# Late mix, joint biases, and weights placed behind the gathers in a four-stage float32 megakernel

## The chip, the cores and the metric

The kernel runs on one core of one Trainium2 chip, as one launch. The time is the device time in microseconds (us) of that core. In the text TensorE is the matrix engine (PE in the profile, PEld its weight loads), VectorE is DVE, ScalarE is ACT, GpSimd is POOL and SyncE is SP, which issues most transfers.

## The reference

Two layers, each a condition network and a feed-forward network with a residual. There are 32 sequences of 128 tokens of width 512, that is 4096 rows. In short:

```python
# L0_cond: two shared matrices and a routed mixture, 8 experts, two per token
shared = (silu(x @ sw1.T) * (x @ sw3.T)) @ sw2.T
hid = (shared + sum over the two chosen e of gate_e * gelu(x @ rw1[e].T) @ rw2[e].T) / 3
# L0_ffn: one expert of 8 for each SEQUENCE, chosen from its last row
sel = argmax(softmax(gelu(hid[:, -1] @ Wp1 + bp1) @ Wp2 + bp2))
r = gelu(hid @ W1[sel] + b1[sel]) @ W2[sel] + b2[sel]
x = x + hid + 0.3 * (r @ Wo + bo)
# L1_cond: mix with the row before, 16 experts by a hash of the token, at most 256 rows each
xprev = rows of x moved down by one, the condition row first
xk = x + (xprev - x) * time_maa_k
xr = x + (xprev - x) * time_maa_r
y = rows of (relu(xk[expert's rows] @ w_key[e]) ** 2) @ w_value[e], put back by token
z = sigmoid(xr @ w_recept.T) * y
# L1_ffn: a recurrence over the 32 sequences (128 tokens side by side)
for t in range(32):
    f, i = sigmoid(z[t] @ wf.T + c @ uf.T + bf), sigmoid(z[t] @ wi.T + c @ ui.T + bi)
    g = tanh(z[t] @ wc.T + c @ uc.T + bc)
    c = f * c + i * g
out = x + tanh(z @ wo.T + c @ uo.T + bo)
```

All is float32. Each matrix product is made of three products of a high and a low part (high by high, high by low, low by high). So every operand is first split: ScalarE casts to the high part (line 63) and VectorE subtracts it to get the low part (line 64).

## The kernel before

**Order.** The program is written as tiles and instructions. A planner fixes each engine's order ahead of the run, from the order in which the program is written and its own estimate of durations; what is written first comes first where both are ready by that estimate. On the chip each engine then takes its instructions in that fixed order. `with tc.issue_after(i)` keeps the instructions written inside it that run on i's engine behind i; it says nothing of other engines. `behind(both)` does so for a pair, one of ScalarE and one of VectorE. `last_split` is the pair of the latest split. A tile pool with `bufs=n` gives n places to tiles of one tag; a tile waits until the place's last user is done, and pools opened later reuse the memory of closed ones.

**Stages.** Up to 300 us: the shared network of the first half of the groups, and the router. Then the routed experts by row blocks, to 560. Then the shared network of the second half (`shared`, L215), in which `combine` (L747) puts the parts together and stores hid. In its last group, after chunk 0, `policy` (L770) chooses the expert of each of the first 24 sequences and sorts them by expert. The first three weights of the next stage are fetched then (`fetch_w`, L859, an indirect gather on POOL), and split in the last three chunks by `hook2` (L939 to 948). Each split is followed by the fetch of the weight three places on, which needs the place of the split one.

**The sequence feed-forward loop** (L1178 to 1237) runs over b from -1 to 32, a sequence b per iteration, with up one block ahead and the rest behind. In iteration b TensorE makes `up(b+1, "a")` (pu), `turn_r(b-1)` (pr: transposes of the finished block), `down(b, "a")` (po), `bend(b+1, "a")` (pt: transposes, then gelu with bias into hf, split into hb), `up(b+1, "b")`, `down(b, "b")`, `bend(b+1, "b")`. `used()` after each product runs `split_w`, inside a condition that is false where the expert stays the same, and fetches the next. `turn_r` adds the bias b2 to pr in PSUM, four 128-column pieces, each once on ScalarE (L1079) and once on VectorE (L1080). In odd iterations `send_k` transposes xk (ptB) and stores its rows; after `down(b, "b")` and after `bend(b+1, "b")` come two `send_v` (pv: xr by w_recept, then the rows are stored to v_d). In even iterations `close` (L1086) multiplies by Wo (pb), adds the residual, makes x1, dx and xk for two sequences, and `mix_r` (L1134) makes xr from dx directly after. Transposes pt, pr, ptB and pth share two PSUM banks (`ps_t`, L976); pb and pv share three. Four late `combine` (pth) and a second `policy` for the last 8 sequences run between iterations 3 and 17. Stores to xk_d and v_d have row addresses that are known only in the run, so each waits for the landing of the one before to the same array.

After the loop come the last `send_k` and `send_v`, with all stores on SyncE.

**The hashed experts** (L1245 to 1387): 16 experts of 8 weight pieces. `fetch_rows` gathers each expert's rows of xk from memory (rowsD), once all xk are stored; `turn_rows` transposes (ptD) and splits them. phD and poD are the two products. The results go to res_d.

**The recurrence** (from L1390): `get_y` gathers y by token from res_d on POOL and loads the gate product r from v_d; `gate_y` multiplies, transposes (ptF) and splits to z; `from_c` and `from_x` make the three gates' products. Its weights come through `weight` (L1373): two halves loaded into staging tiles, then split. uf is loaded on SyncE, wc, wi and wf on ScalarE's queue, into a staging pool of four 4 KB tiles that lies behind the recurrence weights. Eight result tiles (zok) are kept in a pool of their own.

Of the kernel before, what the change touches and what calls it, by code (L numbers as in the profile page):

```python
# [48 lines left out]
def tile_kernel(ctx: ExitStack, tc: tile.TileContext, a: dict, out: bass.AP):  # L49
# [106 lines left out]
    with ExitStack() as sa:  # L156
# [718 lines left out]
        def bias_of(kind, b, o):  # L875
            return bcol[b][:, BIAS[kind] * KD + o : BIAS[kind] * KD + o + 1]
# [21 lines left out]
        with ExitStack() as s2:  # L898
# [65 lines left out]
    with ExitStack() as sb:  # L964
# [37 lines left out]
        def seq(p):  # L1002

            if p not in seqs:
                seqs[p] = nc.sync.value_load(seq_i[0:1, p : p + 1], min_val=0, max_val=PARTS[where(p)[0]] - 1)
            return seqs[p]

        def rows_of(t, p):

            return t[bass.ds((seq(p) + where(p)[0] * PARTS[0]) * P, P), :]  # L1010
# [58 lines left out]
        def turn_r(b):  # L1069
# [7 lines left out]
            for o in range(KD):  # L1077
                hi = rTs[c][:, 0, o, bass.ts(j, P)]
                done_a = nc.scalar.activation(hi, pt[:, o, :], AF.Identity, bias=bias_of("W2a", b, o))  # L1079
                done_v = nc.vector.scalar_tensor_tensor(  # L1080
                    rTs[c][:, 1, o, bass.ts(j, P)], pt[:, o, :], bias_of("W2a", b, o),
                    hi.bitcast(F32), ALU.add, ALU.subtract,
                )
            return done_a.ins, done_v.ins
# [63 lines left out]
        def send_k(b):  # L1148
# [5 lines left out]
            done = nc.scalar.copy(rows, pt.rearrange("p k q -> p (k q)"))  # L1154
            nc.sync.dma_start(out=rows_of(xk_d, b), in_=rows)
            return done.ins
# [21 lines left out]
        for b in range(-1, NB + 1):  # L1178
            c, j = divmod(b - 1, PB)
            if b + 1 < NB:  # L1180
# [28 lines left out]

            pair = b - 3 if b % 2 and 0 <= b - 3 < NB - 2 else None  # L1210
# [15 lines left out]
            if pair is not None and pair < NB - 6:  # L1226
                send_v(pair)
            if b + 1 < NB:
                bend(b + 1, "b")
            if pair is not None and pair < NB - 6:  # L1230
                send_v(pair + 1)
            if j == PB - 1 and 0 <= c < NB // PB:
                wo_done, k_done = close(c, b == NB)
                fetch_xh(c + 1)
                if c < NB // PB - 2:
                    mix_r(c, bp, "xr")
                elif c == NB // PB - 2:
                    mix_r(c, end_p, "xr")
# [3 lines left out]
        for b in range(NB - 2, NB):  # L1242
            rows_done = send_k(b)
# [11 lines left out]
    with ExitStack() as sd:  # L1255
# [97 lines left out]
        for p in range(NPC):  # L1353
# [14 lines left out]
            if p == NPC - 9:  # L1368
# [4 lines left out]
                def weight(name, pool, stage, bufs, tag="raw", parts=2, queue=nc.sync):  # L1373

                    pair = pool.tile([P, 2, KD * D], FR, tag=name, name=f"{name}_hl")
# [14 lines left out]
    with sf:  # L1390
        kw = dict(reuse_waits="tile")
        ZS = 2
        uf_p = sf.enter_context(tc.tile_pool(name="uf_p", bufs=1, side="right", **kw))
# [12 lines left out]
        def get_y(b):  # L1406

            y = yp.tile([P, D], F32, tag="y", name=f"y_{b}")
            nc.gpsimd.indirect_dma_start(  # L1409
# [5 lines left out]
            ys[b] = (y, r)  # L1415

        LEAD = 2
        for b in range(LEAD):
            get_y(b)
# [3 lines left out]
        def gate_y(b):  # L1423
# [11 lines left out]
            split(zs[g][:, 0, :, s], zs[g][:, 1, :, s], pt)  # L1435
# [9 lines left out]
        def from_x(t, ps, which, start, stop):  # L1445
            g, j = divmod(t, GB)
            for n in which:
                if start:
                    ps[n] = ps_g.tile([P, D], F32, tag="g", name=f"ps_{n}_{t}")
                mm3(ps[n], lambda h, k: zs[g][:, h, k, bass.ts(j, P)], lambda h, k: wx[n][:, h, k, :], KD, start, stop)  # L1450

        def from_c(t, n, ps, cT, start, stop):
            if start:
                ps[n] = ps_g.tile([P, D], F32, tag="g", name=f"ps_{n}_{t}")
            mm3(ps[n], lambda h, k: cT[:, h, k, :], lambda h, k: uc[n][:, h, k, :], KD, start, stop)
# [16 lines left out]
        def unit(n, k0=0, k1=KD):  # L1472
# [15 lines left out]
            elif g >= NG - 1 - ZS:  # L1488
                zos[g, o] = zop.tile([P, GT], F32, name=f"zok_{g}_{o}")
# [37 lines left out]
        with tc.tile_pool(name="stage", bufs=4, side="right", **kw) as stage:  # L1527
            uc["f"] = weight("uf", uf_p, stage, 4)
# [198 lines left out]
```

## Time and profile before

| what | value |
|---|---|
| median of 3 runs | 2526.67 us (2520.85 to 2529.47) |
| the profiled execution | 2522.89 us, span 2521.2 us |
| TensorE busy | 2455.6 us (97%) |
| VectorE, ScalarE busy | 1331.5 us (53%), 1064.6 us (42%) |
| mean granted clock of TensorE | 0.989 |
| transfers | 351.11 MB, mean 139 GB/s |

The page lists busy time and instructions of each engine. A wait is listed as who waited, for whom, the total, how often and the longest. In a listing by time, a row has the start, the length from the first to the last instruction merged in it, the engine, line, operation, output and inputs, sizes and count; idle time of the engine before it and what ended it stand in brackets. A stage row has the window, its length, and for each engine the busy time and instructions, then the granted clock, the share of the transfer engines and GB/s.

### The profile page before, as it was taken

Reading aid. Unit: us, or ns where it says so; the run is one execution under the profiler, and the core shown is the slowest. Engines: PE = TensorE matmul, PEld = TensorE weight load, DVE = VectorE, ACT = ScalarE, POOL = GpSimd, SP = SyncE. Lnnn points to the kernel's source line nnn. Section 1 sums busy time; section 2 is a strip of 40 time slices with the busy share of each in tenths; the row PEclk is TensorE's granted clock in tenths of the full one; section 3 lists DMA queues with packets and bytes.
Section 4 is the critical chain, followed back from the end, with each engine's and each line's share of the span. In section 5 each row is a group of like instructions: output and inputs, shape, how many; then the busy total and the mean of one; then the engine's idle time right before and its main releaser. Section 6 shows DMA issues by size and latency. Waiting matters only on the chain. (4 is left out here: it accounts for less than half of the span.)

```text
span 2521.2 us, 37055 instructions
## 1 busy us (share of the span) xinstructions
PE 2455.6 (97%) x13044; PEld 2074.9 (82%) x13044; DVE 1331.5 (53%) x2341; ACT 1064.6 (42%) x1935; POOL 429.6 (17%) x460
## 2 busy tenths in 40 slices
PE   8999999999999899999999999999999999999996
PEld 5688899987888788888887889999978888888885
DVE  7797644556567444444454477667643323333336
ACT  4444533343223555455455466666532212222224
POOL 1000022222233333323223010000010000000003
PEclk9999999999999999999999999999999999999998
DMA  5545544457565333342342387776441111111027
GB/s 180 165 125 168 180 151 154 156 184 249 176 217 168 113 107 127 116 134 70 104 146 96 123 295 226 231 234 224 139 160 42 38 38 38 43 42 42 25 80 267
DMA packets 193117, 351.11 MB, mean 139 GB/s; under 512 B 37473, under 2 KB 72337, under 8 KB 189857
## 3 DMA queue, kind: packets, MB, share of 16 engines
q1 hardware_dynamic: 141504, 244.42, 29.6%
q0 software_dynamic: 36160, 74.90, 10.3%
q10 hardware_dynamic: 15264, 29.37, 3.2%
q8 instruction: 108, 1.77, 0.3%
q14 instruction: 81, 0.66, 0.1%
HBM read 373.94 MB, written 88.13 MB: 183 GB/s over the span
## 5 line engine op out<-in xcount | busy, mean ns | idle before, releaser
L64 DVE TENSOR_TENSOR wD<-rawD,wD 128x1024 fp32r<-128x1024 f32 x128 | 156.4, 1229 | 77.4 <-ACT wD L63 77.2
L81 PE MATMUL p<-xhl,swu 128*128 128x512 f32 x768 | 188.0, 396 | 5.5 <-ACT xhl L63 5.5
L81 PEld LDWEIGHTS phD<-xe,wD 128*128 128x128 f32 x1536 | 184.6, 189 | 1.2
L81 PE MATMUL phD<-xe,wD 128*128 128x256 f32 x1536 | 185.3, 281 | 0.0
L81 PE MATMUL p<-xhl,kept_u 128*128 128x512 f32 x768 | 184.3, 394 | 0.7 <-DVE kept_u L64 0.7
L81 PE MATMUL poD<-wD,hD 128*128 128x512 f32 x768 | 181.3, 392 | 0.0
L81 PEld LDWEIGHTS p<-xhl,swu 128*128 128x128 f32 x768 | 143.8, 189 | 36.0 <-ACT xhl L63 5.8
L81 PEld LDWEIGHTS p<-xhl,kept_u 128*128 128x128 f32 x768 | 141.8, 188 | 30.1 <-DVE kept_u L64 1.1
L81 PEld LDWEIGHTS poD<-wD,hD 128*128 128x128 f32 x768 | 142.0, 188 | 28.4
L63 ACT CAST wD<-rawD 128x1024 fp32r<-128x1024 f32 x128 | 133.1, 1046 | 53.4 <-PE poD L81 48.7
L278 POOL DMA_INDIRECT xg<-in_x_rows_dram,blk_t x71 | 67.6, 952 | 463.4 <-PE ptx L288 257.8
L1409 POOL DMA_INDIRECT y<-res_d,gat_i x32 | 33.3, 1040 | 573.9 <-DVE r L1428 495.2
L81 PE MATMUL pur<-r,xb 128*128 x852 | 118.2, 288 | 0.7 <-DVE xb L64 0.4
L81 PE MATMUL por<-r,hbr 128*128 x426 | 116.3, 407 | 1.4 <-ACT hbr L63 1.3
L64 DVE TENSOR_TENSOR xb<-ptx,xb 128x512 fp32r<-128x512 f32 x71 | 49.1, 692 | 115.3 <-ACT xb L63 115.3
L81 PEld LDWEIGHTS pur<-r,xb 128*128 128x128 f32 x852 | 105.2, 189 | 1.7 <-ACT xb L63 0.7
L81 PE MATMUL ps_f<-wf_hl,z 128*128 128x512 f32 x384 | 96.5, 399 | 0.0
L81 PE MATMUL poF<-z,wo_hl 128*128 128x512 f32 x384 | 96.4, 399 | 0.0
L81 PE MATMUL acc<-swd,as 128*128 128x512 f32 x384 | 96.0, 395 | 0.0
L81 PE MATMUL ps_c<-wc_hl,z 128*128 128x512 f32 x384 | 95.1, 395 | 0.7 <-ACT z L63 0.7
L81 PE MATMUL pb<-rT,Wo_hl 128*128 128x256 f32 x768 | 94.6, 281 | 0.0
L81 PE MATMUL pv<-w_recept_hl,xr 128*128 128x512 f32 x384 | 94.3, 395 | 0.0
(1014 smaller groups left out, 5038.3 us busy)
## 6 DMA issues: line engine op xcount, KB each, us to landing
rawD<-in_w_key_dram SPq DMA_DIRECT2D x64, 512.0 KB, 4.1
rawD<-in_w_value_dram SPq DMA_DIRECT2D x64, 512.0 KB, 3.8
swr<-in_sw_dram SPq DMA_DIRECT2D x120, 256.0 KB, 3.7
o_d<-obr SPq DMA_DIRECT2D x71, 256.0 KB, 2.4
xraw<-in_x_dram SPq DMA_DIRECT2D x32, 256.0 KB, 3.8
rraw<-in_rw_dram SPq DMA_DIRECT2D x32, 256.0 KB, 3.4
xc<-in_x_dram SPq DMA_DIRECT2D x32, 256.0 KB, 3.5
hid_d<-o ACTq DMA_DIRECT2D x32, 256.0 KB, 2.2
```

What stands on the lines that cost most here:

```text
L63: first = nc.scalar.copy(hi, src).ins
L64: done = nc.vector.tensor_tensor(lo, src, hi.bitcast(F32), ALU.subtract).ins
L81: done = nc.tensor.matmul(ps, lhsT=left(hl, k), rhs=right(hr, k), start=start and k + n == 0, stop=stop and 3 * k + n == last,)
L278: nc.gpsimd.indirect_dma_start(out=xg[i], out_offset=None, in_=a["x_rows"], in_offset=bass.IndirectOffsetOnAxis(ap=blk_t[:, i : i + 1], ax ...
L1409: nc.gpsimd.indirect_dma_start(out=y, out_offset=None, in_=res_d, in_offset=bass.IndirectOffsetOnAxis(ap=gat_i[:, b : b + 1], axis=0),)
```

## The change

1. `hook2`: the first three weight splits run in chunks 4, 5 and 6 of the last group, before in 5, 6 and 7.
2. `turn_r`: one VectorE add of all four bias columns into the tile `ps`, then a normal split of the whole block.
3. `mix_r(c)` moves from after `close(c)` to the next odd iteration, behind the split of hb.
4. The two `send_v` of a pair move from the odd iteration to the next even one, around `turn_r` and `down(b, "a")`.
5. `send_k` of the last two sequences issues its stores on ScalarE; later ScalarE work of the tail waits behind that issue, before behind the copy of the rows. The row address is loaded into a register of the issuing engine.
6. Recurrence: a pool of four 4 KB tiles (`zop`) is opened first and serves as staging and later for pairs of zok. The tiles of wi, wf, wc are placed in the order i, f, c. Load order is wc, uf, wi on SyncE, before uf on SyncE and wc, wi, wf on ScalarE. wf is loaded on POOL behind the second gather of y. `gate_y` is no longer held behind wc's first part. The f product of t=0 stays behind c and i, and wo's splits behind z.
7. Two late `load_part` (three transfers) stand inside `issue_after(late)`.

```diff
-                    if c >= KF - AHEAD:
+                    if 4 <= c < 4 + AHEAD:
                         with behind(act_split):
-                            split_w(c - KF + AHEAD)
+                            split_w(c - 4)
...
-            for o in range(KD):
-                hi = rTs[c][:, 0, o, bass.ts(j, P)]
-                done_a = nc.scalar.activation(hi, pt[:, o, :], AF.Identity, bias=bias_of("W2a", b, o))
-                done_v = nc.vector.scalar_tensor_tensor(
-                    rTs[c][:, 1, o, bass.ts(j, P)], pt[:, o, :], bias_of("W2a", b, o),
-                    hi.bitcast(F32), ALU.add, ALU.subtract,
-                )
-            return done_a.ins, done_v.ins
+            rT = ps.rearrange("p (k q) -> p k q", k=KD)
+            bias = bias_of("W2a", b, 0, KD).unsqueeze(2).to_broadcast([P, KD, P])
+            nc.vector.tensor_tensor(rT, pt, bias, ALU.add)
+            s = bass.ts(j, P)
+            split(rTs[c][:, 0, :, s], rTs[c][:, 1, :, s], rT)
+            return tuple(last_split)
...
-            done = nc.scalar.copy(rows, pt.rearrange("p k q -> p (k q)"))
-            nc.sync.dma_start(out=rows_of(xk_d, b), in_=rows)
-            return done.ins
+            nc.scalar.copy(rows, pt.rearrange("p k q -> p (k q)"))
+            return queue.dma_start(out=rows_of(xk_d, b, queue), in_=rows).ins
...
+            gated = b - 4 if b % 2 == 0 and 0 <= b - 4 < NB - 6 else None
+            if gated is not None:
+                send_v(gated)
             if 0 <= b - 1 < NB:
                 r_done = turn_r(b - 1)
             if 0 <= b < NB:
                 down(b, "a")
                 used()
+            if gated is not None:
+                send_v(gated + 1)
...
+            if j == 0 and 0 < c < NB // PB:
+                with behind(last_split) if b + 1 < NB else nullcontext():
+                    mix_r(c - 1, end_p if c == NB // PB - 1 else bp, "xr")
...
-            if pair is not None and pair < NB - 6:
-                send_v(pair)
             if b + 1 < NB:
                 bend(b + 1, "b")
-            if pair is not None and pair < NB - 6:
-                send_v(pair + 1)
             if j == PB - 1 and 0 <= c < NB // PB:
                 wo_done, k_done = close(c, b == NB)
                 fetch_xh(c + 1)
-                if c < NB // PB - 2:
-                    mix_r(c, bp, "xr")
-                elif c == NB // PB - 2:
-                    mix_r(c, end_p, "xr")
...
-            rows_done = send_k(b)
+            rows_done = send_k(b, nc.scalar)
...
+        zop = sf.enter_context(tc.tile_pool(name="zop", bufs=4, side="right", **kw))
         uf_p = sf.enter_context(tc.tile_pool(name="uf_p", bufs=1, side="right", **kw))
...
-        with tc.tile_pool(name="stage", bufs=4, side="right", **kw) as stage:
-            uc["f"] = weight("uf", uf_p, stage, 4)
-            for b in range(LEAD):
-                nc.scalar.activation(ys[b][1], ys[b][1], AF.Sigmoid)
-            for n in "cif":
-                from_c(0, n, ps, cT, True, False)
-            wx["c"] = weight("wc", wx_p, stage, 4, queue=nc.scalar)
-            with tc.issue_after(first_part["wc"]):
-                gate_y(0)
-                gate_y(1)
-            for b in range(LEAD):
-                get_y(b + LEAD)
-            for n in "if":
-                wx[n] = weight("w" + n, wx_p, stage, 4, queue=nc.scalar)
-        zop = sf.enter_context(tc.tile_pool(name="zop", bufs=1, **kw))
+        wx_hl = {n: wx_p.tile([P, 2, KD * D], FR, tag="w" + n, name=f"w{n}_hl") for n in "ifc"}
+        wx["c"] = weight("wc", wx_p, zop, 4, pair=wx_hl["c"])
+        uc["f"] = weight("uf", uf_p, zop, 4)
+        wx["i"] = weight("wi", wx_p, zop, 4, pair=wx_hl["i"])
+        for b in range(LEAD):
+            nc.scalar.activation(ys[b][1], ys[b][1], AF.Sigmoid)
+        for n in "cif":
+            from_c(0, n, ps, cT, True, False)
+        gate_y(0)
+        z_done = gate_y(1)
+        with tc.issue_after(first_got):
+            wx["f"] = weight("wf", wx_p, zop, 4, pair=wx_hl["f"], queue=nc.gpsimd)
+        for b in range(LEAD):
+            get_y(b + LEAD)
...
-                from_x(0, ps, "cif", False, True)
-                wo1 = weight("wo", keep_p, yp, 2, "zo", KD)
+                done = from_x(0, ps, "ci", False, True)
+                with tc.issue_after(done):
+                    from_x(0, ps, "f", False, True)
+                with tc.issue_after(z_done):
+                    wo1 = weight("wo", keep_p, yp, 2, "zo", KD)
...
-                load_part(first_p, "c0", "x", 3, 0)
-                load_part(first_p, "cT0", "x", 3, 1, 2)
+                with tc.issue_after(late):
+                    load_part(first_p, "c0", "x", 3, 0)
+                    load_part(first_p, "cT0", "x", 3, 1, 2)
```

More of the change, by code (lines that the diff above doesn't have):

```diff
@@ L873, in fetch_w, with bias_of @@
                     )
-        def bias_of(kind, b, o):
-            return bcol[b][:, BIAS[kind] * KD + o : BIAS[kind] * KD + o + 1]
+        def bias_of(kind, b, o, n=1):
+            return bcol[b][:, BIAS[kind] * KD + o : BIAS[kind] * KD + o + n]
         def split_w(i):
@@ L1000, in tile_kernel, with seq, rows_of @@
         seqs, end_p = {}, None
[L1002 to L1010, printed above, removed]
+        def seq(p, queue=nc.sync):
+            if (p, queue) not in seqs:
+                seqs[p, queue] = queue.value_load(
+                    seq_i[0:1, p : p + 1], min_val=0, max_val=PARTS[where(p)[0]] - 1
+                )
+            return seqs[p, queue]
+        def rows_of(t, p, queue=nc.sync):
+            return t[bass.ds((seq(p, queue) + where(p)[0] * PARTS[0]) * P, P), :]
         xs = {}
@@ L1146, in mix_r, with send_k @@
             split(xrs[c][:, 0], xrs[c][:, 1], dx)
-        def send_k(b):
+        def send_k(b, queue=nc.sync):
             c, j = divmod(b, PB)
@@ L1371, in tile_kernel, with weight @@
                 uc, first_part = {}, {}
-                def weight(name, pool, stage, bufs, tag="raw", parts=2, queue=nc.sync):
-                    pair = pool.tile([P, 2, KD * D], FR, tag=name, name=f"{name}_hl")
+                def weight(name, pool, stage, bufs, tag="raw", parts=2, queue=nc.sync, pair=None):
+                    if pair is None:
+                        pair = pool.tile([P, 2, KD * D], FR, tag=name, name=f"{name}_hl")
                     flat = a[name].rearrange("p k n -> p (k n)")
@@ L1408, in get_y @@
             y = yp.tile([P, D], F32, tag="y", name=f"y_{b}")
-            nc.gpsimd.indirect_dma_start(
+            got = nc.gpsimd.indirect_dma_start(
                 out=y, out_offset=None, in_=res_d,
@@ L1415, in get_y @@
             ys[b] = (y, r)
+            return got.ins
         LEAD = 2
         for b in range(LEAD):
-            get_y(b)
+            first_got = get_y(b)
         zp = sf.enter_context(tc.tile_pool(name="zp", bufs=2, **kw))
@@ L1434, in gate_y @@
             s = bass.ts(j, P)
-            split(zs[g][:, 0, :, s], zs[g][:, 1, :, s], pt)
+            return split(zs[g][:, 0, :, s], zs[g][:, 1, :, s], pt)
         def turn(c, t):
@@ L1449, in from_x @@
                     ps[n] = ps_g.tile([P, D], F32, tag="g", name=f"ps_{n}_{t}")
-                mm3(ps[n], lambda h, k: zs[g][:, h, k, bass.ts(j, P)], lambda h, k: wx[n][:, h, k, :], KD, start, stop)
+                done = mm3(ps[n], lambda h, k: zs[g][:, h, k, bass.ts(j, P)], lambda h, k: wx[n][:, h, k, :], KD, start, stop)
+            return done
         def from_c(t, n, ps, cT, start, stop):
@@ L1454, in from_c @@
                 ps[n] = ps_g.tile([P, D], F32, tag="g", name=f"ps_{n}_{t}")
-            mm3(ps[n], lambda h, k: cT[:, h, k, :], lambda h, k: uc[n][:, h, k, :], KD, start, stop)
+            return mm3(ps[n], lambda h, k: cT[:, h, k, :], lambda h, k: uc[n][:, h, k, :], KD, start, stop)
         def gate(t, n, ps, v, bias):
@@ L1488, in unit @@
             elif g >= NG - 1 - ZS:
-                zos[g, o] = zop.tile([P, GT], F32, name=f"zok_{g}_{o}")
+                if o % 2 == 0:
+                    zok = zop.tile([P, 2, GT], F32, tag="raw", name=f"zok_{g}_{o}")
+                    zos[g, o], zos[g, o + 1] = zok[:, 0, :], zok[:, 1, :]
                 nc.scalar.copy(zos[g, o], po)
@@ L1554, in tile_kernel @@
                 for n in "cif":
-                    from_c(t, n, ps, cT, False, True)
+                    late = from_c(t, n, ps, cT, False, True)
                     gate(t, n, ps, v, bias)
```

## The prediction

> **What bounds the kernel now.** I read the page, then TensorE's own waits, then the busy time by stage, then the order of time on each engine around every wait. The page first:
>
> ```profile
> span 2521.2 us, 37055 instructions
> PE 2455.6 (97%) x13044; PEld 2074.9 (82%) x13044; DVE 1331.5 (53%) x2341; ACT 1064.6 (42%) x1935; POOL 429.6 (17%) x460
> ```
>
> TensorE is busy in all but 2521.2 - 2455.6 = 65.6 us. Its last matmul ends 21.6 us before the span does, so 44 us are gaps inside. Nothing in the change takes away a matmul, so the gain is in gaps. TensorE's waits, who waited for whom (total, times, longest):
>
> ```profile
> PE pt_0a L1050 <- ACT ue_0a L1043: 7.0, 1, 7.0
> ...
> PE ptD L1304 <- DMA rowsD<-xk_d,slot_t: 3.9, 3, 1.7
> ...
> PE ptF L1433 <- DVE z L64: 2.9, 1, 2.9
> PE pt_6a L1050 <- ACT o L756: 2.6, 1, 2.6
> PE ptB L1152 <- ACT hf_26a L1053: 2.5, 1, 2.5
> PE pt_15a L1050 <- DVEq L891: 2.1, 1, 2.1
> PE ptB L1152 <- ACT hf_16a L1053: 2.0, 1, 2.0
> ```
>
> Stage sums (us, busy of PE, PEld, DVE, ACT, POOL, granted clock, DMA) tell where they lie: the first row is the sequence feed-forward loop, the second the recurrence, which has no gap.
>
> ```profile
> 860.00:1425.00 565.00, 552.48 (x2983) 467.40 (x2982) 261.33 (x501) 293.69 (x658) 171.63 (x169) 0.99 0.33 106
> 1869.00:2462.00 593.00, 593.00 (x2726) 490.30 (x2725) 186.92 (x271) 123.69 (x207) 24.55 (x26) 1.00 0.14 45
> ```
>
> After each large gap the granted clock is 0.50 for a while (same columns):
>
> ```profile
> 842.34:852.58 10.24, 5.40 (x15) 4.44 (x16) 3.61 (x4) 6.74 (x11) 3.81 (x3) 0.50 0.83 310
> 941.33:944.74 3.41, 3.29 (x10) 2.81 (x11) 2.38 (x8) 2.20 (x9) 2.45 (x3) 0.50 0.26 84
> 1135.89:1139.30 3.41, 3.41 (x14) 2.82 (x12) 2.47 (x5) 2.11 (x5) 1.90 (x3) 0.50 0.29 107
> 1327.04:1330.45 3.41, 3.41 (x13) 2.75 (x12) 1.94 (x3) 3.13 (x7) 0.23 (x2) 0.50 0.23 77
> 1460.16:1466.98 6.82, 5.11 (x25) 4.73 (x24) 5.32 (x6) 6.19 (x7) 3.46 (x4) 0.50 0.81 266
> 1845.86:1852.69 6.83, 4.67 (x13) 3.89 (x14) 3.93 (x5) 1.63 (x2) 1.71 (x1) 0.50 0.99 334
> ```
>
> Half of TensorE's busy time in such a stretch is lost on top of the gap. So the four places that the change touches hold:
> - start of the feed-forward loop: 6.96 + 5.40/2 = 9.7
> - the loop: gaps 12.5 (565 - 552.5) + (3.29 + 3.41 + 3.41)/2 = 17.6
> - start of the experts: gaps 0.62 + 1.60 + 1.72 = 3.9, + 5.11/2 = 6.5
> - start of the recurrence: gaps 0.15 + 0.68 + 2.92 + 0.57 = 4.3, + 4.67/2 = 6.6
>
> That is 40.4 us, the ceiling.
>
> **What the Trainium skill says.** (1) "TensorE: Matmul & The Clock Gate", Part 1: the clock falls to half after an idle window and the window, 3413 ns, runs freely; the trace agrees (stretches of 3.41, 6.8 and 10.24 us, after gaps of 2.0 to 7.0 us, though gaps of 2.0 suffice here). (2) "PSUM — Partial Sum Buffer", PSUM bank collisions: ScalarE and VectorE must not read one bank at once, so software orders them. That is the ping-pong of the biases below, 0.79 us a pair. (3) "DMA: Bandwidth & Descriptors", Two DMAs through the same engine are not ordered: the issuing engine has to wait for the first landing. The trace shows 2.0 us of it between the last two stores of xk. (4) Same page, Issuing engines are not separate DMA queues: moving a store to ScalarE saves queueing, not the transfer.
>
> **The change, part by part.**
>
> *Splits one chunk sooner.* ScalarE, by time:
>
> ```profile
> 845.38 1.04 ACT L63 CAST wB_W2b<-rawB 128x1024 fp32r<-128x1024 f32 x1 [7.39 <-DMA rawB<-in_W2b_dram,idxw]
> 846.54 0.59 ACT L1043 COPY ue_0a<-pu_0a 128x512 f32<-128x512 f32 x1
> ```
>
> The cast waits for the fourth weight, and ue_0a, ready since 838.7, stands behind it. That weight was fetched at 835.70, after the split of the third, and took 9.66 us among the loads of the new stage. A chunk is 8.16 us, so it is fetched at 827.5, when only W1b's 2.1 us fetch ran, and lands by 833 to 837. The three weights now split at chunks 4 to 6 landed by 807.3, and chunk 4's split falls at 808.7: no wait. ScalarE and VectorE have room there (5 us idle of each 8). After it, ue_0a is done at 839.4 and TensorE asks for it at 840.2. Gain 7 to 9.7, taken 9.4.
>
> *Joint biases.* Each of 32 blocks had 4 ScalarE (0.37) and 4 VectorE (0.35) instructions in turn:
>
> ```profile
> 1380.31 0.37 ACT L1079 ACTIVATE rT<-pr,b 128x128 fp32r<-128x128 f32 x1 [0.42 <-DVE rT L1080]
> ```
>
> 4 x 0.79 = 3.2 us of a PSUM bank and of ScalarE's order. Now one VectorE add (0.69, the row of v_c from PSUM, same size), one ScalarE cast (0.6), one VectorE subtract (0.69). VectorE keeps 1.4 us, ScalarE falls from 1.5 + 1.26 idle to 0.6, and the bank is free after the first. This bank is what pt_6a, pt_15a and the ptB waits lack: there are two, and one sat behind rT, the other behind work stuck in ScalarE's order.
>
> *Late mix.* mix_r (VectorE 4 x 0.42 = 1.67, ScalarE cast 1.05, VectorE 1.23) leaves the place right after close, where ScalarE idled 2.09 to 3.27 us for it ahead of rT and hf. It goes behind hb of the next odd iteration. What waits for it is send_v, now after up of the following iteration. The distance: pu_b 2.75, ptB 0.7, po 2.85, pt 0.36, pu_a 2.75 = 9.4 us from pt_a; the chain: hf 1.15, hb 0.6 + 0.7, mix 1.67 + 1.05 + 1.23 = 6.4, with hand-overs some 7. Slack 2.4 us. A weight split between (VectorE 2.4) uses it up. The casts of wB in time order show 4 changes of weight inside the loop (at blocks 7, 16, 24, 27): W1's splits of two and W2's of the other two fall into odd iterations (5, 25; 15, 23). I take 0.5 us each.
>
> *Gate products moved.* pv (2 x 2.85) goes from odd to even iterations: TensorE's work becomes 13.7 us odd, 24 even. Blocks 29 and 31 had 13.7 us before and lost 0.34. ScalarE then has about 7.8 us, VectorE 6.4 + 3 left over from close: room, except with splits (4.1 and 4.8). It also puts 5.7 us between ue_a and pt_a where the weights of an even iteration split. Loop together: the four large gaps 9.2 + clock 5.1 go, the small 0.3s (3.3) stay, less 2.0 new: gain 12.3, between 0 and 17.6.
>
> *Last stores on ScalarE.* Before, of the queues' own waits:
>
> ```profile
> SPq L1155 <- DMA xk_d<-rows: 2.0, 1, 2.0
> ```
>
> That is SyncE's wait from 1440 to 1465 for the first of the two stores; POOL's first gather by time:
>
> ```profile
> 1454.08 0.98 POOL L1291 DMA_INDIRECT rowsD<-xk_d,slot_t  x1 [21.43 <-DMA xk_d<-rows]
> ```
>
> The rows were copied by 1446.7, but the first store left SyncE at 1448.36, behind x1's and v's. From ScalarE it leaves at 1446.3, lands about 1448.7; the second about 1450.9; gathers start at 1451.7, 2.4 us sooner. Behind ScalarE's 2.0 us wait stand the cast of xr (1.05) and v's copies: xr is done at 1451.5, pv wants it at 1451.2, 0.3 lost. The two register loads (0.28 + 0.15 each) find idle time. Two of the three ptD waits go; then ScalarE's casts of xe and wD bound: phD at about 1460.4 in place of 1463.4. Gain 3, between 0 and 5.
>
> *Recurrence weights.* VectorE stood in order behind the second gather:
>
> ```profile
> 1845.54 0.69 DVE L1428 TENSOR_TENSOR r<-y,r 128x512 f32<-128x512 f32 x1 [2.55 <-DMA y<-res_d,gat_i]
> ```
>
> It took 6.46 us beside wc, wi and biases (DMA 0.99 busy). Now wc, uf and wi come over SyncE into buffers meant to be free earlier, and wf follows the gathers on POOL. If they load once the last expert's phD ends (1823), all three are split before 1834 (6 casts of 1.05) and the gathers run alone in about 3.5 us: z at 1843.6, TensorE free at 1842.7. 1.3 to 1.6 us remain: gain 5. If the places are free no sooner than uf's cast now (1837.7), gain 0, or -2 for wc, uf and wi in one queue. I take 5, since the order i, f, c puts wc where w_key pieces lie. Biases for t=0 come later on POOL (about 1850) but the first gate's chain has until 1859.
>
> Sum: 9.4 + 12.3 + 3 + 5 = 29.7, so 2522.9 (profiled execution: span 2521.2 and 1.7 around it) becomes 2493. That execution is 3.8 below the median of the runs, 2526.7; on its scale 2497. Edits at nothing: the two load_part behind `late` are issued by SyncE, which an order on TensorE does not touch; wo's splits behind z hide under 20 us of recurrence step; zok pairs keep their memory.
>
> **Rivals.** (1) The loop gives nothing: odd iterations grow new waits as long as the old. For: 2.4 us of slack, VectorE at 9.4 of 13.7. Against: blocks 29 and 31. 17.4 us remain, 2509. (2) The starts give little, transfers only collide elsewhere (DMA 0.7 busy at each), the loop holds: gain about 15, 2512. (3) Slower: xr is late in all 14 odd iterations. One mechanism: VectorE, with close's remains and mix in 13.7 us, delays xr by more than its slack, and TensorE waits at pv. At 2.0 us each, with the clock halved after half of them (1.7), 28 + 12 = 40 lost against 17 won: 2549. It decides once each wait passes 1.8 us: 14 x 1.8 = 25 = 17.4 + 7.6. (4) Parts cancel to about no change, 2525, which includes that the weights are not sooner and the loop even.
>
> **How the numbers follow.** Forecast 0.64 (own range 2487 to 2506), rival (1) 0.15, (2) 0.08, (4) 0.06, (3) 0.07. A change under 0.3% (7.6 us) can't be told from none here: the three runs spread over 8.6. Faster = 0.64 + 0.15 + 0.08 = 0.87; same 0.06; slower 0.07. The range from 2484 (nearly the ceiling) to 2517 holds the forecast, (1) and (2), and leaves out about 0.15.
>
> **What would show it.** pt_0a without a wait and the clock whole at 842; no pt or ptB wait over 1 us in the loop; one VectorE add per block from pr; pv after pu_a without a wait for xr; gathers of rowsD within 5.5 us of the last rows copy; wc, uf, wi cast before 1834's counterpart, z within 1.5 us of ps_f. Waits of pv on xr, or of hb on VectorE behind mix, would prove it wrong.

## The result, and the profile after

The changed kernel takes 2502.35 us in the median of 4 runs (2499.24 to 2503.14), the kernel before 2524.09 us beside it (2520.85 to 2529.47). The ratio is 0.991, with a 95% interval of 0.9892 to 0.9929: 18 to 27 us saved, where the forecast had 29.7. The profiled execution took 2503.14 us, against 2522.89 before. Its page begins:

```profile
span 2501.5 us, 36884 instructions
...
PE 2447.8 (98%) x13044; PEld 2072.3 (83%) x13044; DVE 1334.6 (53%) x2277; ACT 1041.1 (42%) x1839; POOL 417.2 (17%) x462
```

The span is 19.7 us shorter, TensorE's busy time 7.8 us (2455.6 to 2447.8) at the same 13044 matmuls. Most of that is clock: TensorE's busy time at half clock fell from 28.6 to 16.3 us, and half of the difference is 6.1. The rest of the gain is waits. TensorE's own waits in the changed kernel (for whom it waited, total, times, longest):

```profile
PE po L81 <- DVE hb_0a L64: 5.5, 1, 5.5
...
PE phD L81 <- ACT wD L63: 3.3, 1, 3.3
...
PE ptF L1438 <- DVE r L1433: 2.1, 1, 2.1
...
PE pt_6a L1052 <- DVE ps L1082: 0.6, 1, 0.6
PE ptB L1153 <- DVE ps L1082: 0.5, 1, 0.5
PE pv L81 <- ACTq L891: 0.4, 1, 0.4
```

The four waits of the loop (pt_6a, ptB twice, pt_15a) are gone; the longest wait left in the loop is 0.6 us. At each of the three starts one wait is gone and another has come: hb_0a for ue_0a, phD for two of the ptD, r for z in front of ptF. The stages, with the same columns as in the prediction (window, length, busy of PE, PEld, DVE, ACT, POOL, granted clock, share of the transfer engines, GB/s): the loop, the recurrence, and the stretches at half clock.

```profile
860.00:1425.00 565.00, 562.60 (x3093) 479.89 (x3091) 276.59 (x468) 276.12 (x575) 158.99 (x169) 1.00 0.36 115
1852.00:2445.00 593.00, 593.00 (x2726) 490.19 (x2725) 187.17 (x273) 123.58 (x207) 24.62 (x26) 1.00 0.14 45
846.31:853.14 6.83, 3.51 (x8) 2.82 (x9) 3.40 (x5) 0.00 (x0) 2.84 (x3) 0.50 0.39 107
1440.23:1443.64 3.41, 3.41 (x18) 3.23 (x17) 3.41 (x4) 3.41 (x5) 2.52 (x3) 0.50 0.82 219
1453.88:1457.29 3.41, 3.41 (x16) 3.41 (x17) 3.29 (x4) 3.41 (x6) 0.00 (x0) 0.50 0.87 298
1825.93:1832.76 6.83, 6.01 (x18) 4.63 (x19) 2.74 (x5) 2.85 (x4) 3.71 (x5) 0.50 1.02 340
```

In the loop 2.4 us of 565 are left as gaps (12.5 before) and no stretch at half clock (three before). The stretches at the starts are all still there, a little to the side.

To set runs side by side, each is cut at the same TensorE instructions of its listing by time: the start of the loop from the first pu_0a to the first pu_2a, the loop from there to the end of the last pv, the experts' start from there to the first poD, and the recurrence from the first ps_c to the last matmul. Of what lies ahead of pu_0a the edits touch only the first weight splits. Its length varied (833 to 842 us with the sooner splits, 836 to 844 without), more than most of the differences sought, so stages are compared and not spans alone. All in us; ratios are to the kernel before, run on the same chip, with the 95% interval. The medians are from more than one chip, so it is the ratios that compare:

| kernel | start of loop | loop | experts' start | recurrence | median | ratio |
|---|---|---|---|---|---|---|
| before | 27.8 | 593.3 | 19.7 | 665.4 | 2524.09 | |
| changed | 25.5 | 576.4 | 22.0 | 664.1 | 2502.35 | 0.991 (0.9892 to 0.9929) |
| splits sooner, alone | 27.3 | 591.4 | 19.4 | 665.8 | 2525.43 | 1.0002 (0.9993 to 1.0011) |
| joint biases, alone | 26.6 | 584.6 | 20.5 | 665.6 | 2515.43 | 0.9954 (0.9937 to 0.997) |
| late mix and gates moved | 28.0 | 591.0 | 19.3 | 666.5 | 2521.64 | 0.999 (0.9982 to 0.9997) |
| joint biases and late mix | 25.9 | 587.2 | 20.8 | 666.2 | 2521.44 | 0.9977 (0.9969 to 0.9984) |
| joint biases and gates moved | 26.4 | 583.2 | 20.7 | 666.3 | 2514.90 | 0.995 (0.9932 to 0.9968) |
| all three loop parts | 28.2 | 576.5 | 19.9 | 665.5 | 2506.93 | 0.992 (0.9903 to 0.9937) |
| changed, combine later | 18.1 | 585.0 | 19.7 | 663.6 | 2504.66 | 0.992 (0.9903 to 0.9938) |
| changed, stores on SyncE | 26.9 | 576.4 | 18.6 | 666.9 | 2502.79 | 0.991 (0.9892 to 0.9929) |
| changed, wD six ahead | 28.1 | 576.4 | 15.7 | 664.0 | 2500.28 | 0.9903 (0.9884 to 0.9921) |
| changed, wo behind gathers | 26.3 | 576.4 | 19.5 | 667.5 | 2508.46 | 0.9938 (0.9914 to 0.9962) |
| changed, three mends | 18.8 | 576.4 | 16.9 | 664.3 | 2500.64 | 0.9895 (0.9876 to 0.9914) |
| the same, r held back | 18.6 | 576.7 | 15.7 | 660.1 | 2495.15 | 0.9877 (0.986 to 0.9893) |

The rows show how far one profile of a stage can be trusted. With the start of before, the start of the loop took 25.9 to 28.2 us; with that of the changed kernel 25.5 to 28.1. So the 2.3 us that the two first profiles seem to show there are no gain that can be told, and neither are the 2.3 us that they show lost at the experts' start: the same code took 19.7 and 19.5 in other runs. The loop of the kernel before took 593.3 us, and the same loop 591.4 in the run with the splits alone, where one stretch at half clock fell in it and not three; so 2 us of loop in a single profile are no gain either. The time between the first poD and the recurrence was 357.3 to 357.7 us in all rows, that behind the last matmul 21.5 to 22.1.

### The profile page after: what moved, and what is told of

It is laid out like the page before. It is cut to its first block, busy times and chain, and to the rows that moved or that the text cites. A ratio compares the mean times of both kernels' runs of the same rounds, so it can differ in the third digit from the quotient of the medians.

```text
span 2501.5 us, 36884 instructions
## 1 busy us (share of the span) xinstructions
PE 2447.8 (98%) x13044; PEld 2072.3 (83%) x13044; DVE 1334.6 (53%) x2277; ACT 1041.1 (42%) x1839; POOL 417.2 (17%) x462
## 3 DMA queue, kind: packets, MB, share of 16 engines
q1 hardware_dynamic: 141792, 245.99, 29.7%
## 4 chain that ended last, share of the span: by engine, by line
PE 49%; DVE 2%; DMA 1%; issue 0%; ACT 0%; POOL 0%; SPq 0%; POOLq 0%; DVEq 0%; ACTq 0%
PE phD L81 7%; PE ps_f L81 7%; PE ps_c L81 7%; PE ps_i L81 7%; PE poD L81 7%; PE poF L81 3%; PE po L81 3%; PE pb L81 2%; PE pv L81 2%; PE ptC L1445 1%; PE ptF L1438 1%; PE ptD L1305 1%; DMA rawD<-in_w_key_dram 0%; DMA bi_bc<-in_bi_dram 0%; PE ptB L1153 0%
## 5 line engine op out<-in xcount | busy, mean ns | idle before, releaser
L81 PE MATMUL acc<-kept_d,as 128*128 128x512 f32 x384 | 92.8, 390 | 0.6 <-ACT as L63 0.4
```

The source lines that it names most:

```text
L81: done = nc.tensor.matmul(ps, lhsT=left(hl, k), rhs=right(hr, k), start=start and k + n == 0, stop=stop and 3 * k + n == last,)
```

## The experiments

### Which part gains: the loop's parts and the splits, one by one

**Splits one chunk sooner, alone** (the kernel before, with this edit):

```diff
-                    if c >= KF - AHEAD:
+                    if 4 <= c < 4 + AHEAD:
                         with behind(act_split):
-                            split_w(c - KF + AHEAD)
+                            split_w(c - 4)
```

> The kernel before with nothing but the three weight splits one chunk sooner. Theory A (the stall at the start of the loop only moves on to the next late thing, VectorE's late combine that waits for its shared rows from memory ahead of hb_0a): pt_0a no longer waits, TensorE waits about 5.5 us for hb_0a instead of 7.0 for ue_0a, from the first pu to the third 25.5 us instead of 27.8, total about 2 us less. Rival B (the forecast's sum, 9.4 us at this place, and the loss in the changed kernel comes from another part of it): pt_0a and hb_0a both in time, about 9 us less.

Nothing is gained: 1.0002. TensorE's waits have the new first line, in place of 7.0 us for ue_0a:

```profile
PE po L81 <- DVE hb_0a L64: 6.5, 1, 6.5
```

Theory A holds in kind, with less than its 2 us; the forecast's 9.4 is excluded. What VectorE does ahead of hb_0a is seen in its order of time in the changed kernel (start, length, engine, line, operation, and in brackets the idle time before it and what ended it):

```profile
847.25 0.75 DVE L750 SCALAR_TENSOR_TENSOR o<-o,g,shc 128x512 f32<-128x512 f32 x1 [8.82 <-DMA shc<-sh_d]
848.22 0.75 DVE L751 SCALAR_TENSOR_TENSOR o<-o,g,o 128x512 f32<-128x512 f32 x1 [0.21 <-DVEq L891]
848.89 0.68 DVE L64 TENSOR_TENSOR hb_0a<-hf_0a,hb_0a 128x512 fp32r<-128x512 f32 x1
```

VectorE stands idle for 8.82 us in front of the first late `combine`, which is written in iteration 5 and which the planner put ahead of hb_0a. Its shc is stored to sh_d by the shared network's last group and loaded back, and lands at 847. The low part of hb_0a, for which ScalarE's cast ends at 841.6, stands behind it in order. In the kernel before the same two adds stood at the same place, and the wait for the fourth weight hid most of theirs:

```profile
851.39 0.81 DVE L750 SCALAR_TENSOR_TENSOR o<-o,g,shc 128x512 f32<-128x512 f32 x1 [2.06 <-DMA shc<-sh_d]
```

**Joint biases, alone** (the edit of `turn_r` shown in the change).

> The kernel before with nothing but the joint bias add in turn_r. Theory A (the four large waits of the loop come from the ping-pong on one of two PSUM banks and from ScalarE's order behind it, so this part alone takes most of them away): total 8 to 13 us less, the waits pt_6a, pt_15a and the two of ptB all under 1 us. Rival B (they come from xr's work right after close, which holds ScalarE): total 0 to 4 us less, at least three of the four waits still over 1.5 us.

```profile
PE pt_6a L1050 <- DVEq L891: 2.2, 1, 2.2
PE ptB L1151 <- DVEq L891: 2.1, 1, 2.1
PE pt_15a L1050 <- DVE ps L1080: 1.4, 1, 1.4
```

Some 12 us of the total (8 to 16 by the interval). But only one of the four large waits is gone, to 0.5 us (ptB in front of block 16), and one is smaller (pt_15a, 2.1 to 1.4); the other two are only 0.4 us shorter. So theory A has the size and not its reason: beside the large waits most of the small ones went too. Of the 8.7 us that the loop lost, 5.0 are gaps (12.5 to 7.5). The rest is TensorE's busy time, 580.7 to 577.2, which is two of its three half-clock stretches. The run with the splits alone lost two of them as well, with all four waits in place, so this rest can't be put down to the edit; the last section shows what it hangs on.

**Late mix and gate products moved, without the joint biases.**

> The kernel before with the late mix and the moved gate products, biases in four pieces as before. Theory A (ping-pong on the bank is the cause): 2 to 6 us less, waits of pt or ptB of over 1 us remain in the loop, perhaps at other blocks. Rival B (xr's work after close is the cause): 10 to 15 us less, no wait over 1 us in the loop. If it is slower, the moved work alone makes new waits, which the joint add then pays for.

```profile
PE ptB L1152 <- DVE rT L1080: 7.0, 8, 3.6
...
PE pt_6a L1050 <- DVE rT L1080: 2.3, 1, 2.3
```

The total is some 3 us less (1 to 4.5 by the interval); the 2.3 us of the loop are no more than its spread. Now the large waits are for rT, the four pieces on VectorE and ScalarE in turn, which hold the bank that ptB and pt_6a need; one has grown from 2.0 to 3.6 us.

**All three.**

> The kernel before with all three parts in the loop (joint biases, late mix, gate products moved), starts as before. Theory A (the loop carries the gain, the three starts together give about 1 us): 16 to 19 us less, loop of 576 us instead of 593, starts as before to within 1 us. Rival C (the starts give as forecast, 17 us, and the loop's 17 hide a shift of time between the stages): 12 us less or under.

The loop takes 576.5 us, as in the changed kernel, and the total is within its interval. The parts are worth more together (16.8) than the sum of the two runs above (8.7 + 2.3), and so they are in gaps alone, which no half-clock stretch blurs: 10.2 us of gaps are gone, against 5.0 and 2.5. The totals point the same way (20 us against 12 and 3), but with intervals too wide to show it. Two more runs divide the second of them, each with joint biases: the late mix with the gates in their old places, and the gates moved with the mix in its old place.

> The kernel before with joint biases and late mix, gate products in their old places (odd iterations), so that they come in the iteration that also makes xr. Theory A (the move of the gates only gives xr time, without it TensorE waits at pv for xr in most odd iterations): slower than with joint biases alone, 2518 to 2545. Rival B (late mix alone brings what the joint add leaves, and the gates' place is indifferent): 2506 to 2509, loop 576 to 579 us.

> The kernel before with joint biases and the gate products moved, xr made right after close as before. Theory A (late mix is what frees ScalarE's order around close; moving the gates alone adds little to the joint add): 2511 to 2515, loop 581 to 585 us. Rival B (the gates' place is what fills TensorE where the weights of an even iteration split, the waits pt_6a and ptB that the joint add left): 2506 to 2509, loop 576 to 579 us.

Late mix on top of the joint biases makes the loop slower, 587.2 against 584.6, and the total too (0.9977 against 0.9954, with intervals that barely overlap). In that run TensorE waits in front of pv, which needs xr (ScalarE's branch around a weight split, L891, is named as what came last):

```profile
PE pv L81 <- ACTq L891: 4.3, 3, 2.0
```

The long ones are two, 1.91 us in iteration 5 and 1.97 in iteration 25, both with a change of weight. The gaps are no longer than with joint biases alone (7.5 us each), and each loop has one half-clock stretch; it is TensorE's busy time that is 2.5 us longer. Short waits are not in that list. They show in the waits of the weight loads, which run just ahead of their matmuls (830 to 1430 us):

```profile
PEld pv L81 <- ACTq L891: 5.5, 3, 2.4
PEld pv L81 <- DVEq L891: 2.5, 8, 0.5
PEld pv L81 <- ACT xr L63: 1.2, 2, 0.6
PEld pv L81 <- DVE xr L64: 1.1, 3, 0.5
```

These 16 waits lie in 12 of the 13 odd iterations with gate products; with joint biases alone there is none of them. At each, a part of xr ends some 0.05 us before the load starts. The first matmul behind such a load takes 0.50 us, where pv otherwise takes 0.24 a matmul. There are 14 of these at full clock, so by estimate they cost 14 x 0.26 = 3.6 us, which covers the 2.5. So theory A is right, "most odd iterations" too, though most of the waits are short.

Gates moved on top of joint biases leave pt_6a at 2.2 us and ptB at 2.1 and take away the 1.4 us of pt_15a; the total can't be told from that with joint biases alone. Neither edit is worth much alone: with xr made right after `close`, pt_6a and ptB wait for work in ScalarE's and VectorE's order; with xr made late they wait only 0.6 and 0.5 us, but with the gates not moved pv waits for xr. Only the pair takes both away.

### Why the starts gave nothing

**The start of the loop.** The four late combines are written behind hb of their own iteration:

```diff
-            if 0 <= late < GB and step == 2:
-                combine(NB - GB + late, ps_t)
             if b + 1 < NB:
                 bend(b + 1, "a")
+            if 0 <= late < GB and step == 2:
+                with behind(last_split):
+                    combine(NB - GB + late, ps_t)
```

> The changed kernel with the late combines written behind hb of their own iteration (5, 8, 11, 14), so that VectorE does not take the first of them ahead of hb_0a. Theory A (the stall at the start of the loop moved to this combine, which waits for shared rows that come from memory): hb_0a without its wait of 5.5 us, start of the loop 18 to 20 us instead of 25.5, about 6 to 7 us less than the changed kernel in all, 2495 to 2497. Rival B (the start is limited by the transfers themselves, the next weight or hb_0b is then late by as much): start stays at 24 to 26, total within 2 us of the changed kernel's 2502.

The start falls to 18.1 us, 7.4 less than in the changed kernel: here theory A is shown right. TensorE goes straight into po (by time):

```profile
845.36 1.17 PE L81 MATMUL pu_1a<-wB_W1a,hidhl 128*128 128x512 f32 x4
846.37 2.91 PE L81 MATMUL po<-wB_W2a,hb_0a 128*128 128x512 f32 x12
```

And yet nothing is gained in the total, since the loop took 8.7 us more. TensorE now meets the combine's transposes right behind its adds:

```profile
PE pth L754 <- DVE o L751: 6.4, 4, 3.6
```

Two of the four waits, 3.57 and 2.22 us, were followed by half-clock stretches. The adds had to leave the front of hb_0a, but not to come so close to their transposes.

**The experts' start.** Two runs on the changed kernel. In the first the last two stores of xk go back to SyncE (`send_k(b)` in place of `send_k(b, nc.scalar)`):

> The changed kernel with the last two stores of xk back on SyncE. Theory A (rows come sooner but the experts' start then stands at the casts of wD in order on ScalarE and VectorE, whose seventh piece is loaded late, so the store's place gives nothing): from the last pv to the first poD 20 to 22 us as before or a little less, total within 2 us of 2502. Rival B (the earlier gathers do give 2 to 3 us and something else took them): 2 to 3 us slower, 24 to 25 us from pv to poD.

The total is the same. Rows come later here, but nothing else waits:

```profile
1443.66 0.63 PE L1305 MATMUL ptD<-ident,rowsD 128*128 128x128 f32 x4 [1.58 <-DMA rowsD<-xk_d,slot_t]
1445.61 0.97 PE L1305 MATMUL ptD<-ident,rowsD 128*128 128x128 f32 x5 [1.32 <-DMA rowsD<-xk_d,slot_t]
...
1447.21 12.81 PE L81 MATMUL phD<-xe,wD 128*128 128x256 f32 x94
```

In the changed kernel the first phD starts 3.6 us after the last pv (1439.88), here 5.1 us (1446.34); that is the sooner gather. But in the changed kernel phD stops after 72 matmuls, and ScalarE, VectorE and TensorE show why, in this order:

```profile
1450.80 1.05 ACT L63 CAST wD<-rawD 128x1024 fp32r<-128x1024 f32 x1 [2.05 <-DMA rawD<-in_w_value_dram]
1451.75 0.59 ACT L1322 ACTIVATE rl<-phD 128x512 f32<-128x512 f32 x1
```

```profile
1451.88 1.23 DVE L64 TENSOR_TENSOR wD<-rawD,wD 128x1024 fp32r<-128x1024 f32 x1 [2.84 <-ACT wD L63]
1453.02 0.68 DVE L1324 TENSOR_TENSOR hf<-rl,phD 128x512 f32<-128x512 f32 x1
```

```profile
1453.85 4.61 PE L81 MATMUL phD<-xe,wD 128*128 128x256 f32 x24 [3.25 <-ACT wD L63]
```

The splits of the seventh and eighth weight piece wait for their loads. hf, which frees the first of three PSUM banks of phD, stands behind the eighth on VectorE and ends at 1453.70, just before phD goes on. The page puts this wait down to ScalarE's wD; in the run with the combine later the same stop is put down to hf:

```profile
1455.65 4.59 PE L81 MATMUL phD<-xe,wD 128*128 128x256 f32 x24 [2.30 <-DVE hf L1325]
```

If that reading is right, it is the order that costs, and splitting less far ahead mends it:

```diff
-        AHEAD, RAW = 8, 6
+        AHEAD, RAW = 6, 6
```

> The changed kernel with wD split six pieces ahead of use instead of eight, so that the first relu and its product stand ahead of the seventh cast, which waits for its load. Theory A (this order holds TensorE for 3.25 us and half a clock window): no wait of phD over 1 us, 17.5 to 19 us from the last pv to the first poD instead of 22, total 3 to 5 us less than 2502. Rival B (the loads themselves are late, and pieces 7 to 9 are wanted when they land): the wait moves to a later phD or poD and the total stays within 1 us.

```profile
1444.75 11.41 PE L81 MATMUL phD<-xe,wD 128*128 128x256 f32 x94
```

phD runs through. 15.7 us in place of 19.5 to 22, better than expected, and the pieces that were split ahead of need are not missed: what follows, up to the recurrence, takes 357.6 us, against 357.4 before. The total, 2500.28, can't be told from the changed kernel's; in the profiled execution the start of the loop fell at the long end of its spread (28.1) and hides the stage's gain. The last two runs below have AHEAD at 6 too and show it again (16.9 and 15.7).

**The start of the recurrence.** In the changed kernel wi, the two r and two pieces of wo load while the last expert's results are being stored. POOL's first gather of y, which needs both stores, by time:

```profile
1820.99 1.89 POOL L1413 DMA_INDIRECT y<-res_d,gat_i  x1 [79.85 <-DVE wi_hl L64]
```

The second store was issued at 1816.48, so the gather starts 4.5 us later. In the kernel before, where that store was issued at 1835.01, it was 2.8:

```profile
1837.80 0.95 POOL L1409 DMA_INDIRECT y<-res_d,gat_i  x1 [78.14 <-DMA res_d<-ob]
```

The test loads wo on POOL, behind the first four gathers:

```diff
+            last_got = get_y(b + LEAD)
...
-                    wo1 = weight("wo", keep_p, yp, 2, "zo", KD)
+                with tc.issue_after(z_done), tc.issue_after(last_got):
+                    wo1 = weight("wo", keep_p, yp, 2, "zo", KD, queue=nc.gpsimd)
```

> The changed kernel with the loads of wo on POOL behind the first four gathers of y, before on SyncE ahead of the last stores of res_d. Theory A (wi, r and wo run beside the last two stores of res_d, which land 3.7 to 4.4 us after their issue instead of 2.0, and hold the gathers): stores land in 2.0 to 3 us, first gather starts at about 1819.5 on the changed kernel's clock instead of 1821.0, ptF's wait 0.5 to 1 us instead of 2.1, total 1.5 to 3 us less. Rival B (the gathers take their time whatever runs beside the stores): ptF's wait stays at 2 us, total within 1 us of 2502.

The gather starts 2.9 us after the second store's issue (1816.95), and TensorE finds r done:

```profile
1819.81 1.28 POOL L1413 DMA_INDIRECT y<-res_d,gat_i  x1 [78.21 <-DVE wc_hl L64]
```

```profile
1824.45 0.66 PE L1438 MATMUL ptF<-ident,r 128*128 128x128 f32 x4
...
1846.99 1.12 PE L1445 MATMUL ptC<-ident,c 128*128 128x128 f32 x4 [6.41 <-DVE c L1473]
```

So the transfers did hold the gather, and theory A is right on that wait. All the traces agree: from the store's issue to the gather it is 2.8 to 2.9 us in the seven with the old tail, 4.5 to 6.1 in the four with the changed one, and 2.9 to 3.7 in the three with wo behind the gathers. The second line is the price: VectorE waited 3.33 us in front of the third block's multiply, for its sigmoid on ScalarE, and wo's splits too came between the gates of the first step; c was 6.4 us late. The recurrence took 667.5 us, the longest of all rows. The total is the highest of the runs on the changed kernel, though the interval of its ratio overlaps that of the changed kernel's.

### The mends together

Three mends on the changed kernel: only the two adds of the first combine stand behind hb_1a, its transposes stay in iteration 5; AHEAD is 6; wo is loaded as in the last test and split behind c's transposes of the first step.

```diff
+            if b == 0:
+                get_o(NB - GB, cb, 1)
             if b + 1 < NB:
                 bend(b + 1, "a")
+            if b == 0:
+                with behind(last_split):
+                    add_up(NB - GB)
...
             cT_next = turn(c, t + 1)
+            if t == 0:
+                with behind(last_split), tc.issue_after(last_got):
+                    wo1 = weight("wo", keep_p, yp, 2, "zo", KD, queue=nc.gpsimd)
```

> The changed kernel with three mends: VectorE's two adds of the first late combine stand behind hb_1a (its transposes stay where they were), wD split six pieces ahead, wo loaded and split behind c's transposes of the first recurrence step. Theory A (each start was held by one known late thing, and these three take it away without a new wait): start of the loop 18 us, loop 576, pv to poD 16, recurrence 661 to 662, in all 13 to 17 us less than the changed kernel: 2486 to 2490. Rival B (a stall that is taken away at one start comes back at the next late thing, as it did in the changed kernel): at most 5 us less, 2497 or more.

Start (18.8) and experts' start (16.9) come close to theory A's 18 and 16, so the mends hold there. The recurrence doesn't (664.3), and the total is as rival B has it: 2500.64, or 0.9895 on a chip where the kernel before took 2527.47. A new wait has come, so rival B is right once in three places, and VectorE's order shows whose it is:

```profile
PE ptC L1456 <- DVE c L1484: 2.8, 1, 2.8
```

```profile
1831.98 0.69 DVE L1444 TENSOR_TENSOR r<-y,r 128x512 f32<-128x512 f32 x1 [3.26 <-ACT r L1443]
1832.59 0.69 DVE L1476 TENSOR_TENSOR v_i<-ps_i,bi_bc 128x512 f32<-128x512 f32 x1
```

The fourth block's multiply, not wanted for another 20 us, stands ahead of the second gate of the first step. The last run holds it back:

```diff
-                gate_y(b)
+                with behind(first_cT) if t == 1 else nullcontext():
+                    gate_y(b)
```

> The kernel with three mends, and with the fourth block's gate multiply (r of y) held on VectorE and ScalarE behind c's transposed split of the first recurrence step. Theory A (the new wait of 2.75 us for c in the recurrence comes only from that multiply, which stands ahead of the first gates and waits for its load): no wait of ptC over 0.3 us, recurrence 660.5 to 662 us instead of 664.3, other stages as with three mends (18.8, 576.4, 16.9), ratio to the kernel before 0.987 to 0.989. Rival B (the gates are held by wo's loads or biases all the same): recurrence 663 us or more, ratio 0.989 to 0.991.

```profile
851.88 2.91 PE L81 MATMUL po<-wB_W2a,hb_0a 128*128 128x512 f32 x12
...
1836.09 0.66 PE L1456 MATMUL ptC<-ident,c 128*128 128x128 f32 x4
```

Neither instruction waits. The recurrence takes 660.1 us, the ratio is 0.9877 (0.986 to 0.9893), 27 to 35 us of 2528.15. This is about what the forecast wanted from the change itself. It beats the kernel before; against the changed kernel it was not timed on one chip, and the intervals of the two ratios just touch; but its three starts (with the recurrence) are 7 to 9.5, 4 to 6 and 3.5 to 7 us shorter than in the runs of the changed kernel's code, and the loop is equal.

## Why the prediction was right or wrong

The time lies in the predicted range, and faster was right. The sum was 29.7 us; the two profiles differ by 19.7, and the measured interval (18 to 27) leaves the sum out. That the total came so near is in part luck: the loop gave 4.6 us more than its term, and the three starts, with 17.4 us in the sum, 1.3 by the two profiles. By its steps:

**"Splits one chunk sooner", gain 9.4: wrong, nothing.** Its own links held: the weight landed in time, ue_0a was not late. What failed is "TensorE asks for it at 840.2" as the end of the argument. It asked what ends the wait for ue_0a and not what is late next; VectorE's late combine, with 2.06 us of waiting for shc already in the trace of before and hb_0a behind it, was. The run with this part alone gives 1.0002, and moving the combine as well brings the start to 18 us. The forecast's 9.4 was there to be had, for two edits and not for one.

**The loop, gain 12.3: right in mechanism, too small.** 16.8 with the loop's parts alone, 16.9 in the changed kernel (15 if set against the loop of 591.4). Two terms were mis-sized: "the small 0.3s (3.3) stay" and "less 2.0 new". The gaps fell from 12.5 to 2.4, so 10.1 and not 7.2 net. TensorE's busy time in the loop fell by 6.8 (580.7 to 574.0), where the half-clock stretches account for the forecast's 5.1; the other 1.7 is not settled. The 5.1 is itself the clock of one execution. It is not so that the clock is halved "after each large gap": behind the 2.13 us of pt_15a it was not, and the same loop had one stretch in place of three in the run with the splits alone. What the forecast had as a reason for each wait, "one sat behind rT, the other behind work stuck in ScalarE's order", fits the runs: the joint biases take most of the first kind, the late mix the second (2.2 and 2.1 us fell to 0.6 and 0.5), and the moved gates pay for the late xr. Of the ping-pong itself only one hand-over of the two is an order on the bank: VectorE's instruction also reads ScalarE's result, as its old lines in the change show.

**The 2.0 for late xr** was charged at four weight changes. In the changed kernel only 0.4 us of it came. With the gates in their old places two of those four, iterations 5 and 25, did wait, 1.91 and 1.97, and ten more iterations a little. So the move of the gates is what paid for the late mix.

**"Last stores on ScalarE", gain 3: wrong, nothing.** The gathers are sooner and the ptD waits fell from 3.9 us to 1.6, about as forecast. The step said that "ScalarE's casts of xe and wD bound" and stopped at the first phD. The loads of the seventh and eighth splits, and hf behind these splits, were late next. With the stores back the total is the same (2502.79).

**"Recurrence weights", gain 5: mostly wrong, 1 to 2 in three profiles of four** (663.6 to 664.1 against 665.4 to 666.5; in the fourth, 666.9, the gather came latest, 6.1 us behind the store). The weights were split by 1822, before ps_f ended at 1824, but later than forecast: they were to be done by 1834, which is where ps_c began in the kernel before, and here ps_c began at 1815.7 and the first cast of wc, in order behind the copies of the last results, at 1816.3. Wrong, too, was that then "the gathers run alone in about 3.5 us": the sooner loads, with r and wo behind them in SyncE's queue, ran beside the stores that the gathers wait for. The sum had no term for wo's transfers.

**Rival (2)** had the starts right ("transfers only collide elsewhere", though at two of the three starts it was an order on VectorE) and the loop too small; its 2512 with 16.9 in place of 12.3 is 2507. **Rivals (1) and (3)**, new waits in odd iterations, don't occur in the changed kernel; with the gates in their old places xr is late as (3) has it, in 12 odd iterations of 13, but mostly by far less than its 2.0 us.

## What to carry to other kernels

Before a stall is counted as gained, list all that the waiting instruction's successor needs, with the time at which each is ready, and look for what stands in order ahead of it on every engine: the second-latest decides the gain, and an idle time that ends a little before the stall's end is the sign of it. Edits that free one shared bank or one engine's order are worth their sum only where they remove different last arrivals; here three edits gave 17 us of the loop together, one of them 9 alone and the other two 2 without it. And when work is moved away from the front of something, leave it its distance from what consumes it.

## What the runs showed of the hardware that was not expected

The Trainium skill ("TensorE: Matmul & The Clock Gate", Part 1) says that the clock is halved after an idle window of 3413 ns which runs freely. The free-running window agrees: the stretches at half clock are 3.41 us or multiples of it, and all of one execution start on one grid. In the kernel before they start at 842.34, 941.33, 1135.89 and 1327.04, that is 29, 57 and 56 windows of 3.413 us apart; in each other trace the grid lies elsewhere.

But a wholly idle window isn't needed. What tells is TensorE's idle time within one window of the grid. Counted so between 830 and 2470 us of the fourteen traces, 42 windows at full clock had 1.95 us of it or more, and all 42 were followed by one at half clock; 1022 had some, up to 1.51 us, and none was; of 16 in between 7 were. At half clock, 0.65 us or more was followed by another such window (31 of 31), 0.57 or less by full clock (20 of 20). The ends of matmuls are modelled in a trace, so these limits are rough. So the length of a gap alone doesn't tell. In the run with the splits alone, the 2.60 us in front of pt_6a lay across two windows and cost no clock; the first row is the window with more of the gap. The 1.95 us in front of pt_15a lay within one window, the second row, and the third row follows it (columns as in the stages above, the clock third from the end):

```profile
936.03:939.44 3.41, 1.79 (x10) 1.58 (x11) 2.73 (x7) 2.54 (x8) 2.34 (x3) 1.00 0.21 79
1106.68:1110.09 3.41, 1.46 (x9) 1.17 (x9) 1.91 (x6) 1.85 (x6) 1.52 (x2) 0.99 0.03 3
1110.09:1113.50 3.41, 3.41 (x10) 2.63 (x9) 2.15 (x4) 2.29 (x5) 1.65 (x3) 0.50 0.43 153
```

Shorter gaps in one window count together: 1.36, 1.65 and 1.31 us within 6 us, at the experts' start of the run with joint biases alone, were followed by 6.83 us at half clock. A wait of 2 us thus costs 2 or, with half of a 3.41 us stretch on top, 3.7 us by where it falls, and that differs from one execution to the next.
